# Moving transposes from TensorE to DMA and VectorE (32x32 blocks) in a fused two-layer graph kernel

## The chip, the cores and the metric

The kernel runs on one core of one Trainium2 chip. The metric is the device time of one execution in microseconds (us). The kernel before takes 2777.66 us (median of 3 runs, 2776.79 to 2779.71).

Names of engines in the profile: PE is TensorE's matmul, PEld its weight load, DVE is VectorE, ACT is ScalarE, POOL is GpSimd, SP is SyncE, which issues nearly all DMAs (all but 7 of 534 in the kernel before). A `q` behind an engine's name means its sequencer, which is where DMAs are issued. The granted clock is the share of TensorE's full speed that the profile shows; in the traces here it is either 1.00 or 0.50 (all 14 clock records of the kernel before), and figures between are means.

## The reference, cut to what matters

128 graphs of 128 nodes with 512 features go through an attention layer and a hypergraph layer. Only the first part matters for the change:

```python
# layer 0, per graph b and head h (8 heads of 64 units)
feats = einsum('bnf,hfu->bhnu', x, W)
dense = (feats . a_self)[..., :, None] + (feats . a_neigh)[..., None, :]
dense = leaky_relu(dense, 0.2) + NEG_BIG * (1 - adj)
att   = softmax(dense)                       # over neighbours j
out   = einsum('bhij,bhju->bhiu', att, feats) + b
x     = layernorm(x + relu(out))
# layer 1: y = R @ relu(R @ x @ W1 + b1) ..., R = D^-1 H B^-1 H^T with H = (adj != 0)
```

In this program each product on TensorE sums over the index that lies on the partitions of its operands. So `feats` takes x transposed (`xT`) and the weighted sum over j takes the exponentials transposed (`eT`); the degrees B, which VectorE sums along rows, take adj transposed (`hT`).

## The kernel before

Graphs are handled in 64 pairs. The large products are done with seven half-size products in place of eight; ScalarE copies some of the partial results out of PSUM and VectorE adds them. Each step is registered with a lag (how many pairs behind it works) and a position in the period. The positions are sorted once, and that order is the program order of every engine. The program is unrolled.

```python
    @step(0, 37.9)
    def transposes(p, s):                  # TensorE: x
        ...
                nc.tensor.transpose(t[:, k * P:(k + 1) * P], s["x"][:, g, k * P:(k + 1) * P], ident)
    def x_evict(p, s, g):                  # ScalarE: PSUM -> xT
        nc.scalar.copy(s["xT"][:, g].rearrange("p k n -> p (k n)"), s["pt"][g])
    ...
    @step(2, 21.6)
    def e_transpose(p, s):                 # TensorE: exponentials
        ...
                    nc.tensor.transpose(t[:, h * N:(h + 1) * N], s["nb"][:, g, q * HH + h, :], ident)
    def e_evict(p, s, g, q):               # ScalarE or VectorE: PSUM -> eT
        copy = (nc.scalar.copy, nc.vector.tensor_copy)[q]
        ...
    # what the argument needs besides
    at(3, 17.3, h_sum, 1, 0, 1, "W")       # VectorE: adds two partial results of ph
    at(3, 18.5, relu, 1, 0)                # ScalarE: ReLU of that sum
    # chain("pf", ...): ScalarE's copies of pfX stand behind it in ScalarE's order
    with tc.manual_schedule():
        for t in range(PAIRS + last):
            if 1 < t < PAIRS:
                load(t)
            ...
            for _, fn, args in sorted(todo, key=lambda e: e[0]):
                fn(*args)
```

In the profile `pz`, `ph`, `pf`, `pav`, `pr`, `py` and `pq` are TensorE's products in PSUM; `pf` gives the features, `pav` the weighted sums, `pr` the score rows. `nb` holds the scores, then the exponentials. A letter X, Y or W behind a product's name tells which PSUM bank collects it.

## Time and profile before

| what | kernel before | where it is read |
|---|---|---|
| time | 2777.66 us | median of 3 runs |
| TensorE busy | 98% of the span | busy shares of the page |
| chain of waits | 96% PE | the chain that ended last |
| one period (start of pz to the next) | 41.97 us | chain in order of time |
| busy in one period: PE, DVE, ACT, POOL | 42.0, 28.0, 26.3, 26.7 us | table of stretches |
| share of the DMA engines | 18% | queue table |

The first two rows say that TensorE bounds the kernel. The period turns a saving into a time: a microsecond taken out of every period is worth 64 us, as long as TensorE stays the bound. The lines themselves are in the prediction below.

### The profile page before, as it was taken

What the parts mean: (1) busy time and instruction counts of PE and PEld (TensorE: products, weight loads), DVE (VectorE), ACT (ScalarE), POOL (GpSimd) and SP (SyncE); (2) the same over time, 40 slices, a digit from 0 to 9 for tenths busy, and PEclk for the clock granted to TensorE, in tenths of its full rate; (3) what the DMA queues carried; (4) which work ended last, traced back from release to release, by engine and by line L of the source; (5) the groups of instructions that cost most, each with busy time, mean ns of one, the idle gap of its engine ahead of it and who ended that gap; (6) DMA issues with size and microseconds to landing.
All of it is one profiled execution on the core that took longest, in us unless ns stands there. A gap on an engine that the chain in (4) does not pass through costs nothing.

```text
span 2777.1 us, 50570 instructions
## 1 busy us (share of the span) xinstructions
PE 2713.2 (98%) x18272; PEld 2476.2 (89%) x18272; DVE 1796.3 (65%) x4264; ACT 1689.8 (61%) x4677; POOL 1725.9 (62%) x1813
## 2 busy tenths in 40 slices
PE   5799999999999999999999999999999999999997
PEld 4699999999999999999999999999999999999996
DVE  5566666666666666666666666666666666676663
ACT  2566566566566566666666665665665665665662
POOL 3665665666666666656656656656656656656654
PEclk8899999999999999999999999999999999999999
DMA  5111211211212212211212212212112112112110
GB/s 153 49 61 48 65 55 50 70 49 56 69 43 62 69 43 62 70 43 62 69 43 62 69 43 62 62 50 62 62 49 63 57 48 70 49 56 69 43 39 23
DMA packets 99660, 161.61 MB, mean 58 GB/s; under 512 B 11602, under 2 KB 48466, under 8 KB 99412
## 3 DMA queue, kind: packets, MB, share of 16 engines
q1 hardware_dynamic: 95716, 157.32, 18.0%
q8 instruction: 146, 2.39, 0.4%
q10 hardware_dynamic: 3696, 1.06, 0.2%
q14 instruction: 102, 0.84, 0.1%
HBM read 124.27 MB, written 34.08 MB: 57 GB/s over the span
## 4 chain that ended last, share of the span: by engine, by line
PE 96%; POOL 1%; DMA 1%; issue 1%; ACT 0%; DVE 0%; SPq 0%; POOLq 0%; DVEq 0%; ACTq 0%
PE phX L646 16%; PE pyX L404 16%; PE pfX L404 8%; PE phW L646 8%; PE pav L519 8%; PE pyW L404 8%; PE pz L610 4%; PE pfW L404 4%; PE phY L646 4%; PE pyY L404 4%; PE pq L767 4%; PE pet L498 4%; PE pfY L404 2%; PE pt L312 2%; PE pd L364 1%; PE pa L323 1%
## 5 line engine op out<-in xcount | busy, mean ns | idle before, releaser
L459 POOL TENSOR_TENSOR nb<-nb,neg 128x512 f32<-128x512 f32 x256 | 347.7, 1380 | 92.9 <-DMA nb<-rd 90.9
L646 PEld LDWEIGHTS phX<-zS,w_sb 128*128 128x128 f32 x3072 | 364.5, 193 | 41.2 <-issue 31.3
L646 PE MATMUL phX<-zS,w_sb 128*128 128x128 f32 x3072 | 375.9, 276 | 10.4 <-ACT ph L271 10.4
L271 ACT COPY py<-pyX 128x257 f32<-128x257 f32 (+1 forms) x192 | 71.4, 372 | 501.3 <-PE pyX L404 500.2
L466 ACT ACTIVATE nb<-nb,ft 128x128 f32<-128x128 f32 x1024 | 326.8, 392 | 50.5 <-POOL nb L459 49.5
L697 POOL TENSOR_TENSOR sq<-sq 128x512 f32<-128x512 f32 (+2 forms) x384 | 311.4, 818 | 20.1
L676 ACT ACTIVATE h<-h,b_sb 128x128 f32<-128x128 f32 x768 | 244.6, 391 | 124.3 <-DVE h L661 124.3
L479 ACT ACTIVATE nb<-nb,nm 128x128 f32<-128x128 f32 x1024 | 313.0, 391 | 0.0
L566 POOL TENSOR_TENSOR rso<-veo,mhalf 128x2 f32<-128x2 f32 x64 | 44.9, 701 | 420.9 <-DVE veo L564 420.9
L386 POOL TENSOR_TENSOR hS<-h 128x512 f32<-128x512 f32 x128 | 160.1, 1272 | 180.9 <-ACT h L676 180.9
L404 PE MATMUL pyX<-w_sb,h 128*128 128x257 f32 (+1 forms) x1024 | 252.9, 389 | 0.4 <-ACT py L271 0.2
L404 PE MATMUL pyX<-w_sb,hS 128*128 128x257 f32 (+1 forms) x1024 | 244.5, 381 | 2.5 <-POOL hS L386 2.5
L550 DVE SCALAR_TENSOR_TENSOR y<-y,x 128x512 f32<-128x512 f32 x128 | 186.6, 1458 | 89.4 <-POOL y L543 89.4
L519 PE MATMUL pav<-ft,eT 128*128 128x65 f32 x2048 | 241.8, 273 | 2.0 <-ACT eT L506 1.9
L404 PE MATMUL pyW<-w_sb,hS 128*128 128x256 f32 x1024 | 242.7, 379 | 0.0
L519 PEld LDWEIGHTS pav<-ft,eT 128*128 128x128 f32 x2048 | 239.6, 193 | 2.4 <-ACT eT L506 2.1
L634 POOL TENSOR_TENSOR zS<-zT 128x256 f32<-128x256 f32 x128 | 95.1, 743 | 226.5 <-ACT zT L621 226.5
L404 PEld LDWEIGHTS pyX<-w_sb,hS 128*128 128x128 f32 x1024 | 194.7, 190 | 31.5 <-POOL hS L386 2.9
L404 PEld LDWEIGHTS pyW<-w_sb,hS 128*128 128x128 f32 x1024 | 193.3, 189 | 29.1 <-DVE y L729 1.1
L427 DVE TENSOR_TENSOR ft<-pf,pfW 128x264 f32<-128x264 f32 x128 | 55.0, 430 | 236.5 <-ACT pf L271 165.5
L404 PEld LDWEIGHTS pyX<-w_sb,h 128*128 128x128 f32 x1024 | 185.4, 191 | 21.9 <-ACT py L271 0.7
L472 DVE TENSOR_REDUCE nm<-nb 128x4 f32<-128x512 f32 x256 | 168.7, 678 | 31.0 <-ACT nb L466 30.1
(131 smaller groups left out, 6174.1 us busy)
## 6 DMA issues: line engine op xcount, KB each, us to landing
nb<-rd SPq DMA_DIRECT2D x128, 512.0 KB, 4.5
x<-in_x_dram SPq DMA_DIRECT2D x64, 512.0 KB, 5.7
out_dram<-o SPq DMA_DIRECT2D x64, 512.0 KB, 2.8
a<-in_adj_dram SPq DMA_DIRECT2D x64, 128.0 KB, 5.0
w<-in_adj_dram SPq DMA_DIRECT2D x128, 64.0 KB, 4.8
w_sb<-in_w1t_dram SPq DMA_DIRECT2D x3, 512.0 KB, 6.5
w_sb<-in_w2t_dram SPq DMA_DIRECT2D x3, 512.0 KB, 9.2
w_raw<-in_w_dram SPq DMA_DIRECT2D x4, 256.0 KB, 6.6
```

Of the source, the lines that this page charges most:

```text
L386: engine.tensor_tensor(t[:, i], in0, in1, op=op)
L404: nc.tensor.matmul(to[:, :n], lhs[:, k, :], rhs[:, k, :n], start=bool(start) and k == 0, stop=(k == nk - 1), skip_group_check=True,)
L459: nc.gpsimd.tensor_tensor(t, t, s["neg"][:, g, None, :].to_broadcast([P, HH, N]), op=ALU.add)
L466: nc.scalar.activation(t, t, AF.Prelu, bias=s["ft"][:, g, h, 0:1], alpha=SLOPE)
L472: nc.vector.tensor_reduce(s["nm"][:, g, hs], s["nb"][:, g, hs, :], AX.X, ALU.max, negate=True)
L479: nc.scalar.activation(t, t, AF.Exp, bias=s["nm"][:, g, h:h + 1])
L498: nc.tensor.transpose(t[:, h * N:(h + 1) * N], s["nb"][:, g, q * HH + h, :], ident)
L519: nc.tensor.matmul(t[:, h * (U + 1):(h + 1) * (U + 1)], s["eT"][:, g, q * HH + h, :], s["ft"][:, g, q * HH + h, 2:], start=True, stop=True,)
L550: nc.vector.scalar_tensor_tensor(y, y, 0.0, s["x"][:, g, :], op0=ALU.max, op1=ALU.add)
L646: nc.tensor.matmul(to[:, m * N:(m + 1) * N], w[:, k, m * P:(m + 1) * P], rhs[:, k, :], start=bool(start) and m == 0 and k == 0, stop=(k == ...
L676: nc.scalar.activation(dst[:, k, :], src[:, k, :], AF.Relu, bias=b1_sb[:, c:c + 1])
L697: nc.gpsimd.tensor_tensor(t[:, :n, :], t[:, :n, :], t[:, n:2 * n, :], op=ALU.add)
```

## The change

TensorE spends 2.84 us of each period on the transposes of x, adj and the exponentials. The change takes these away; the small ones of hD and of the score rows stay. x and adj are read twice from DRAM, once in rows and once with the 32x32 blocks already at their transposed places. The exponentials are written to DRAM and read back in the same manner. VectorE then transposes inside each block (0.69 us for 128x512 in the mean of the 256 transposes of the exponentials; every experiment that uses it gave a correct result). Many positions are moved to the new pace. The core of the diff:

```diff
+    def load_blocks(p):
+        s["xb"] = work.tile([P, 2 * NB, P], F32, tag="xb", name=f"xb_{p}")
+        rows = x[gs].rearrange("g (b n) (f c) -> f n (g b) c", b=NB, f=NB)
+        for f in range(NB):
+            nc.sync.dma_start(s["xb"][f * B:(f + 1) * B], rows[f])
+        ...  # the same for adj, into "ab": eight DMAs in all
-    @step(0, 37.9)
-    def transposes(p, s):
-        ...
+    def x_transpose(p, s, g):
+        nc.vector.transpose(s["xT"][:, g]..., s["xb"][:, g * NB:(g + 1) * NB]...)
+    at(1, 4.7, x_transpose, 0)
+    at(1, 5.3, x_transpose, 1)
     ...
+    def e_write(p, s, g):
+        s["ed", g] = dram.tile([P, NB, H * B], F32, tag="ed", name=f"ed_{p}_{g}")
+        nc.sync.dma_start(s["ed", g], s["nb"][:, g * NB:(g + 1) * NB]...)
+    def e_read(p, s, g):
+        s["eb", g] = work.tile([P, NB, H, B], F32, tag="eb", name=f"eb_{p}_{g}", bufs=2)
+        for b in range(NB):
+            nc.sync.dma_start(s["eb", g][b * B:(b + 1) * B]..., s["ed", g][:, b, :]...)
+    def e_transpose(p, s, g, q):
+        nc.vector.transpose(s["eT"][:, g, hs, :]..., s["eb", g][:, :, hs, :]...)
-        ((0, 0), 33.0, (1, 34.9), (1, 37.3), 9.5), ...
+        ((0, 0), 32.7, (1, 33.4), (1, 34.8), 3.0, 12.5), ((0, 1), 34.0, (1, 35.7), (1, 37.3), 4.7, 13.9),
+        ((1, 0), 35.2, (1, 37.9), (2, 2.0), 9.3, 19.8), ((1, 1), 36.4, (1, 39.0), (2, 2.7), 11.6, 20.6),
     ...
+            if 0 < t < PAIRS:
+                todo.append((6.0, load_blocks, (t,)))
```

(The six columns of the table are: which quarter, then the positions of masking, leaky ReLU, maximum, exponential and VectorE's transpose.)

More of the change, by code (lines that the diff above doesn't have):

```diff
@@ L73 @@
     PAIRS = G // 2
+    B = 32
+    NB = P // B
     const = ctx.enter_context(tc.tile_pool(name="const", bufs=1))
@@ L94, in load @@
             nc.sync.dma_start(s["w"][:, g, :], adj[2 * p + g, 0, :].partition_broadcast(P))
-        if p:
-            load_x(p)
-    def load_x(p):
+    def load_blocks(p):
         s = st[p]
-        s["x"] = work.tile([P, 2, F], F32, tag="x", name=f"x_{p}", bufs=3)
-        nc.sync.dma_start(s["x"], x[2 * p:2 * p + 2].rearrange("g n f -> n g f"))
+        gs = slice(2 * p, 2 * p + 2)
+        s["xb"] = work.tile([P, 2 * NB, P], F32, tag="xb", name=f"xb_{p}")
+        rows = x[gs].rearrange("g (b n) (f c) -> f n (g b) c", b=NB, f=NB)
+        for f in range(NB):
+            nc.sync.dma_start(s["xb"][f * B:(f + 1) * B], rows[f])
+        s["ab"] = work.tile([P, 2 * NB, B], F32, tag="ab", name=f"ab_{p}")
+        rows = adj[gs].rearrange("g (b n) (f e) -> f n (g b) e", b=NB, f=NB)
+        for f in range(NB):
+            nc.sync.dma_start(s["ab"][f * B:(f + 1) * B], rows[f])
     load(0)
@@ L119 @@
         raw = work.tile([P, KF // 2, QU], F32, tag=("eT", "nb", "sq", "hS")[2 * i + j], name=f"w0_raw{i}{j}")
-        block(raw, w0, i, j, F // 2, QU)
+        rows = w0.rearrange("(b k f) c -> b f k c", b=NB, k=KF)
+        for b in range(NB):
+            nc.sync.dma_start(
+                raw[b * B:(b + 1) * B],
+                rows[b][:, i * KF // 2:(i + 1) * KF // 2, j * QU:(j + 1) * QU],
+            )
         w0_blocks.append((dst, raw.rearrange("p k (h u) -> p k h u", h=HH), j))
@@ L129 @@
     an_bc = spread(a_neigh, F, "an_bc")
-    load_x(0)
+    load_blocks(0)
     load(1)
@@ L180, in prepare_first @@
                 t = work.tile([P, KF // 2, HH, U], F32, tag=("o", "x")[c], name=f"wa{n}{c}",
-                              bufs=(2, 3)[c])
+                              bufs=2)
                 (nc.vector, nc.gpsimd)[c].tensor_tensor(
@@ L276, in chain @@
             at(lag, t, copy, i)
-    @step(0, 10.4)
+    @step(0, 9.2)
     def nodes(p, s):
@@ L284, in nodes @@
         dd = small.tile([P, 2], F32, tag="dd", name=f"dd_{p}")
-        junk = work.tile([P, N], F32, tag="junk", name=f"junk_{p}")
+        w = s["w"]
         for g in range(2):
             nc.vector.scalar_tensor_tensor(
-                junk, a[:, g, :], 0.0, s["w"][:, g, :], op0=ALU.not_equal, op1=ALU.mult,
+                w[:, g, :], a[:, g, :], 0.0, w[:, g, :], op0=ALU.not_equal, op1=ALU.mult,
                 accum_out=dd[:, g:g + 1],
@@ L299, in nodes @@
             )
-    @step(0, 38.3)
+    @step(0, 38.4)
     def mask(p, s):
@@ L304, in mask, with load_rows @@
         nc.gpsimd.tensor_scalar(s["neg"], s["a"], -1.0, BIG, op0=ALU.add, op1=ALU.mult)
-    @step(0, 37.9)
-    def transposes(p, s):
-        s["pt"] = []
-        for g in range(2):
-            t = bank(f"pt_{p}_{g}")
-            for k in range(KF):
-                nc.tensor.transpose(
-                    t[:, k * P:(k + 1) * P], s["x"][:, g, k * P:(k + 1) * P], ident
-                )
-            s["pt"].append(t)
-    @step(1, 1.75)
+    @step(1, 1.78)
     def transpose_nodes(p, s):
         s["pa"] = bank(f"pa_{p}")
-        for i, t in enumerate((s["a"], s["hD"])):
-            for g in range(2):
-                c = (2 * i + g) * N
-                nc.tensor.transpose(s["pa"][:, c:c + N], t[:, g, :], ident)
-    def x_evict(p, s, g):
+        for g in range(2):
+            nc.tensor.transpose(s["pa"][:, g * N:(g + 1) * N], s["hD"][:, g, :], ident)
+    @step(1, 31.0)
+    def load_rows(p, s):
+        s["x"] = work.tile([P, 2, F], F32, tag="x", name=f"x_{p}", bufs=2)
+        nc.sync.dma_start(s["x"], x[2 * p:2 * p + 2].rearrange("g n f -> n g f"))
+    def x_transpose(p, s, g):
         if g == 0:
             s["xT"] = work.tile([P, 2, KF, N], F32, tag="xT", name=f"xT_{p}")
-        nc.scalar.copy(s["xT"][:, g].rearrange("p k n -> p (k n)"), s["pt"][g])
-    at(0, 38.5, x_evict, 0)
-    at(0, 39.1, x_evict, 1)
+        nc.vector.transpose(
+            s["xT"][:, g].rearrange("p k (b n) -> p k b n", b=NB),
+            s["xb"][:, g * NB:(g + 1) * NB].rearrange("p b (k f) -> p k b f", k=KF),
+        )
+    at(1, 4.7, x_transpose, 0)
+    at(1, 5.3, x_transpose, 1)
     @step(1, 2.6)
@@ L335, in d_evict @@
         s["hDT"] = work.tile([P, 2, N], F32, tag="hDT", name=f"hDT_{p}")
-        nc.scalar.copy(s["hDT"].rearrange("p g n -> p (g n)"), s["pa"][:, 2 * N:])
-    @step(1, 2.4)
+        nc.scalar.copy(s["hDT"].rearrange("p g n -> p (g n)"), s["pa"][:, :2 * N])
+    @step(1, 3.4)
     def edges(p, s):
@@ L342, in edges @@
         hT = work.tile([P, 2, N], F32, tag="hT", name=f"hT_{p}")
+        nc.vector.transpose(hT.rearrange("p g (b n) -> p (g b) n", b=NB), s["ab"])
         for g in range(2):
             nc.vector.tensor_scalar(
-                hT[:, g, :], s["pa"][:, g * N:(g + 1) * N], 0.0, None, op0=ALU.not_equal,
-                op1=ALU.add, accum_out=deg[:, g:g + 1],
+                hT[:, g, :], hT[:, g, :], 0.0, None, op0=ALU.not_equal, op1=ALU.add,
+                accum_out=deg[:, g:g + 1],
             )
@@ L350, in edges @@
         s["hT"], s["be"] = hT, deg
-    @step(1, 16.5)
+    @step(1, 18.6)
     def scale_edges(p, s):
@@ L358, in scale_edges @@
             )
-    @step(1, 25.15)
+    @step(1, 34.6)
     def propagator(p, s):
@@ L367, in propagator @@
             )
-    @step(1, 25.9)
+    @step(1, 35.3)
     def r_evict(p, s):
@@ L394 @@
     for i in range(4):
-        at(1, 6.0 + 0.7 * i, x_sums, i)
+        at(1, 6.1 + 0.7 * i, x_sums, i)
     def rows_product(s, i, a, sums, w, n, nk, extra, to, start):
@@ L413, in feature @@
                      w0_sb.rearrange("p b k h u -> p b k (h u)"), FW, KF // 2, 0, to, start)
-    chain("pf", 1, (17.1, 18.0, 18.9, 19.8, 20.7, 23.35, 24.25, 18.15, 19.95, 21.75),
+    chain("pf", 1, (16.2, 17.1, 18.0, 18.9, 19.8, 22.4, 23.3, 17.3, 19.0, 20.8),
           feature, FW)
@@ L427, in f_sum @@
             nc.vector.tensor_tensor(dst, by_head(s["pf", i]), by_head(s["pf", where]), op=ALU.add)
-    at(1, 19.2, f_sum, 0, 0, 0, "Y")
-    at(1, 22.3, f_sum, 1, 1, 2, "W")
-    at(1, 25.3, f_sum, 0, 1, 1, "W")
-    at(1, 24.5, f_sum, 1, 0, None, "X")
-    @step(1, 27.3)
+    at(1, 18.2, f_sum, 0, 0, 0, "Y")
+    at(1, 21.4, f_sum, 1, 1, 2, "W")
+    at(1, 24.4, f_sum, 0, 1, 1, "W")
+    at(1, 23.4, f_sum, 1, 0, None, "X")
+    @step(1, 25.95)
     def transpose_scores(p, s):
@@ L439, in transpose_scores @@
         )
-    @step(1, 27.6)
+    @step(1, 26.2)
     def spread_rows(p, s):
@@ L445, in spread_rows, with neighbours, scores @@
         nc.vector.tensor_copy(rows, s["pr"][:2 * H, :N])
-        rd = dram.tile([2, H, N], F32, tag="rd", name=f"rd_{p}")
-        nc.sync.dma_start(rd.rearrange("g h n -> (g h) n"), rows)
-        s["nb"] = work.tile([P, 2, H, N], F32, tag="nb", name=f"nb_{p}")
+        rd = s["rd"] = dram.tile([2, NB, H, B], F32, tag="rd", name=f"rd_{p}")
         for g in range(2):
             nc.sync.dma_start(
-                s["nb"][:, g].rearrange("p h n -> p (h n)"),
-                rd[g].rearrange("h n -> (h n)").partition_broadcast(P),
-            )
+                rd[g].rearrange("b h j -> h b j"),
+                rows[g * H:(g + 1) * H].rearrange("h (b j) -> h b j", b=NB),
+            )
+    @step(1, 28.0)
+    def neighbours(p, s):
+        s["nb"] = work.tile([P, 2 * NB, H, B], F32, tag="nb", name=f"nb_{p}")
+        for g in range(2):
+            nc.sync.dma_start(
+                s["nb"][:, g * NB:(g + 1) * NB].rearrange("p b h j -> p (b h j)"),
+                s["rd"][g].rearrange("b h j -> (b h j)").partition_broadcast(P),
+            )
+    def scores(s, g, hs):
+        return s["nb"][:, g * NB:(g + 1) * NB, hs, :]
     def masked(p, s, g, q):
-        t = s["nb"][:, g, q * HH:(q + 1) * HH, :]
+        t = scores(s, g, slice(q * HH, (q + 1) * HH))
+        neg = s["neg"][:, g].rearrange("p (b j) -> p b j", b=NB)
         nc.gpsimd.tensor_tensor(
-            t, t, s["neg"][:, g, None, :].to_broadcast([P, HH, N]), op=ALU.add
+            t, t, neg[:, :, None, :].to_broadcast([P, NB, HH, B]), op=ALU.add
         )
@@ L464, in leaky @@
         for h in range(q * HH, (q + 1) * HH):
-            t = s["nb"][:, g, h, :]
+            t = scores(s, g, h)
             nc.scalar.activation(t, t, AF.Prelu, bias=s["ft"][:, g, h, 0:1], alpha=SLOPE)
@@ L472, in largest @@
         nc.vector.tensor_reduce(
-            s["nm"][:, g, hs], s["nb"][:, g, hs, :], AX.X, ALU.max, negate=True
+            s["nm"][:, g, hs], scores(s, g, hs).rearrange("p b h j -> p h b j"), AX.XY,
+            ALU.max, negate=True,
         )
@@ L477, in exponential @@
         for h in range(q * HH, (q + 1) * HH):
-            t = s["nb"][:, g, h, :]
+            t = scores(s, g, h)
             nc.scalar.activation(t, t, AF.Exp, bias=s["nm"][:, g, h:h + 1])
-    for (g, q), tm, (lag, tl), (lagx, tx), te in (
-        ((0, 0), 33.0, (1, 34.9), (1, 37.3), 9.5), ((0, 1), 34.3, (1, 36.2), (1, 38.3), 10.8),
-        ((1, 0), 35.6, (1, 40.6), (2, 3.5), 12.6), ((1, 1), 36.9, (2, 2.9), (2, 4.3), 13.9),
+    def e_write(p, s, g):
+        s["ed", g] = dram.tile([P, NB, H * B], F32, tag="ed", name=f"ed_{p}_{g}")
+        nc.sync.dma_start(
+            s["ed", g], s["nb"][:, g * NB:(g + 1) * NB].rearrange("p b h j -> p b (h j)")
+        )
+    def e_read(p, s, g):
+        s["eb", g] = work.tile([P, NB, H, B], F32, tag="eb", name=f"eb_{p}_{g}", bufs=2)
+        for b in range(NB):
+            nc.sync.dma_start(
+                s["eb", g][b * B:(b + 1) * B].rearrange("p i h j -> p i (h j)"),
+                s["ed", g][:, b, :].rearrange("(b i) x -> i b x", b=NB),
+            )
+    def e_transpose(p, s, g, q):
+        if (g, q) == (0, 0):
+            s["eT"] = work.tile([P, 2, H, N], F32, tag="eT", name=f"eT_{p}")
+        hs = slice(q * HH, (q + 1) * HH)
+        nc.vector.transpose(
+            s["eT"][:, g, hs, :].rearrange("p h (b i) -> p h b i", b=NB),
+            s["eb", g][:, :, hs, :].rearrange("p b h j -> p h b j"),
+        )
+    for (g, q), tm, (lag, tl), (lagx, tx), te, tt in (
+        ((0, 0), 32.7, (1, 33.4), (1, 34.8), 3.0, 12.5), ((0, 1), 34.0, (1, 35.7), (1, 37.3), 4.7, 13.9),
+        ((1, 0), 35.2, (1, 37.9), (2, 2.0), 9.3, 19.8), ((1, 1), 36.4, (1, 39.0), (2, 2.7), 11.6, 20.6),
     ):
@@ L488 @@
         at(2, te, exponential, g, q)
-    @step(2, 21.6)
-    def e_transpose(p, s):
-        for g in range(2):
-            for q in range(2):
-                t = s["pet", g, q] = bank(f"pet_{p}_{g}{q}")
-                for h in range(HH):
-                    nc.tensor.transpose(
-                        t[:, h * N:(h + 1) * N], s["nb"][:, g, q * HH + h, :], ident
-                    )
-    def e_evict(p, s, g, q):
-        if (g, q) == (0, 0):
-            s["eT"] = work.tile([P, 2, H, N], F32, tag="eT", name=f"eT_{p}")
-        copy = (nc.scalar.copy, nc.vector.tensor_copy)[q]
-        copy(
-            s["eT"][:, g, q * HH:(q + 1) * HH, :].rearrange("p h n -> p (h n)"), s["pet", g, q]
-        )
-    at(2, 22.6, e_evict, 0, 0)
-    at(2, 22.75, e_evict, 0, 1)
-    at(2, 23.5, e_evict, 1, 0)
-    at(2, 23.6, e_evict, 1, 1)
+        at(2, tt, e_transpose, g, q)
+        if q:
+            at(2, te + 1.6, e_write, g)
+            at(2, te + 3.6, e_read, g)
     def attend(p, s, g):
@@ L522, in attend @@
                 )
-    at(2, 25.6, attend, 0)
-    at(2, 27.4, attend, 1)
+    at(2, 20.65, attend, 0)
+    at(2, 24.2, attend, 1)
     def attended(p, s, g):
@@ L537, in attended @@
             )
-    at(2, 27.8, attended, 0)
-    at(2, 29.4, attended, 1)
+    at(2, 22.5, attended, 0)
+    at(2, 26.4, attended, 1)
     def add_bias(p, s, g):
         nc.gpsimd.tensor_tensor(s["y"][:, g, :], s["y"][:, g, :], b0_bc, op=ALU.add)
-    at(2, 29.9, add_bias, 0)
-    at(2, 31.2, add_bias, 1)
+    at(2, 24.1, add_bias, 0)
+    at(2, 28.0, add_bias, 1)
     def residual(p, s, g):
@@ L572, in normalize @@
         )
-    at(2, 31.3, residual, 0)
-    at(2, 33.2, residual, 1)
-    at(2, 35.5, rstds, "a")
-    @step(2, 36.3)
+    at(2, 27.6, residual, 0)
+    at(2, 30.0, residual, 1)
+    at(2, 31.7, rstds, "a")
+    @step(2, 32.6)
     def first_shift(p, s):
@@ L589, in first_output @@
         )
-    at(2, 39.7, first_output, 0)
-    at(2, 39.8, first_output, 1)
+    at(2, 37.0, first_output, 0)
+    at(2, 37.1, first_output, 1)
     def skip(p, s, g):
@@ L600, in skip @@
         )
-    at(3, 9.0, skip, 0)
-    at(3, 9.7, skip, 1)
+    at(3, 6.6, skip, 0)
+    at(3, 6.7, skip, 1)
     def propagate(p, s, g):
@@ L620, in z_evict @@
             s["zT"] = work.tile([P, 2, KF, N], F32, tag="zT", name=f"zT_{p}")
+            s["zS"] = work.tile([P, 4, KF // 2, N], F32, tag="zS", name=f"zS_{p}")
         nc.scalar.copy(s["zT"][:, g].rearrange("p k n -> p (k n)"), s["pz", g])
     at(3, 1.1, z_evict, 0)
-    at(3, 1.95, z_evict, 1)
+    at(3, 2.0, z_evict, 1)
     def z_sums(p, s, i):
-        if i == 0:
-            s["zS"] = work.tile([P, 4, KF // 2, N], F32, tag="zS", name=f"zS_{p}")
         b, t = halves(s["zT"], KF // 2), s["zS"]
@@ L634, in z_sums @@
         nc.gpsimd.tensor_tensor(t[:, i], in0, in1, op=ALU.subtract)
-    for i, t in enumerate((2.6, 3.3, 4.0, 4.7)):
+    for i, t in enumerate((2.7, 3.4, 4.1, 4.8)):
         at(3, t, z_sums, i)
@@ L650, in hidden @@
                 )
-    chain("ph", 3, (3.06, 4.81, 6.56, 8.31, 10.06, 13.56, 15.31, 4.9, 8.9, 12.0), hidden,
+    chain("ph", 3, (2.0, 3.8, 5.6, 7.35, 9.1, 12.65, 14.4, 4.0, 7.5, 11.0), hidden,
           HALF)
@@ L663, in h_sum @@
         )
-    at(3, 6.75, h_sum, 0, 0, 0, "Y")
-    at(3, 12.8, h_sum, 1, 1, 2, "W")
-    at(3, 17.3, h_sum, 1, 0, 1, "W")
+    at(3, 5.9, h_sum, 0, 0, 0, "Y")
+    at(3, 11.8, h_sum, 1, 1, 2, "W")
+    at(3, 16.4, h_sum, 1, 0, 1, "W")
     def relu(p, s, g, q):
@@ L676, in relu @@
             nc.scalar.activation(dst[:, k, :], src[:, k, :], AF.Relu, bias=b1_sb[:, c:c + 1])
-    at(3, 15.2, relu, 1, 1)
-    at(3, 16.5, relu, 0, 1)
-    at(3, 18.5, relu, 1, 0)
-    at(3, 7.6, relu, 0, 0)
+    at(3, 12.8, relu, 1, 1)
+    at(3, 14.5, relu, 0, 1)
+    at(3, 17.7, relu, 1, 0)
+    at(3, 8.1, relu, 0, 0)
     def square(p, s, g, q):
@@ L688, in square @@
         )
-    for (g, q), t in (((0, 0), 20.3), ((0, 1), 20.9), ((1, 0), 24.8), ((1, 1), 26.3)):
+    for (g, q), t in (((0, 0), 19.4), ((0, 1), 20.0), ((1, 0), 21.2), ((1, 1), 21.8)):
         at(3, t, square, g, q)
@@ L700 @@
         for level in range(3):
-            at(3, (25.0, 26.3, 27.0)[level] + 2.4 * g, squares, g, level)
+            at(3, (25.4, 26.7, 27.4)[level] + 3.9 * g, squares, g, level)
     def h_sums(p, s, i):
@@ L705, in h_sums @@
                    nc.gpsimd, "hS")
-    at(3, 21.1, h_sums, 0)
-    at(3, 22.4, h_sums, 1)
-    at(3, 19.8, h_sums, 2)
-    at(3, 23.7, h_sums, 3)
+    at(3, 20.3, h_sums, 0)
+    at(3, 21.6, h_sums, 1)
+    at(3, 19.0, h_sums, 2)
+    at(3, 22.8, h_sums, 3)
     def weigh(s, i, to, start):
         rows_product(s, i, halves(s["h"], KH // 2), s["hS"], w2_sb, QU, KH // 2, 1, to, start)
-    chain("py", 3, (29.2, 30.95, 32.7, 34.4, 36.2, 39.2, 40.9, 31.0, 34.5, 38.0), weigh,
+    chain("py", 3, (26.0, 27.8, 29.5, 31.2, 33.0, 35.5, 37.2, 27.9, 31.4, 34.75), weigh,
           QU, 1)
@@ L729, in y_sum @@
             nc.vector.tensor_tensor(dst, s["py", i][:, :n], s["py", where][:, :n], op=ALU.add)
-    at(3, 32.75, y_sum, 0, 0, 0, "Y")
-    at(3, 38.4, y_sum, 1, 1, 2, "W")
+    at(3, 29.6, y_sum, 0, 0, 0, "Y")
+    at(3, 35.4, y_sum, 1, 1, 2, "W")
     at(4, 0.1, y_sum, 0, 1, 1, "W")
-    at(3, 40.2, y_sum, 1, 0, None, "X")
-    @step(3, 38.8)
+    at(3, 37.3, y_sum, 1, 0, None, "X")
+    @step(3, 35.0)
     def sum_squares(p, s):
@@ L742, in sum_squares @@
             )
-    @step(3, 39.3)
+    @step(3, 36.0)
     def h_rstd(p, s):
@@ L769, in output @@
         )
-    at(4, 11.81, output, 0)
-    at(4, 12.7, output, 1)
+    at(4, 10.9, output, 0)
+    at(4, 11.8, output, 1)
     def o_sum(p, s, g):
@@ L779, in o_stats @@
         moments(p, s, "o", s["o"][:, g, :], g)
-    at(4, 13.4, o_sum, 0)
-    at(4, 14.1, o_sum, 1)
-    at(4, 14.8, o_stats, 0)
-    at(4, 15.6, o_stats, 1)
-    at(4, 15.7, rstds, "o")
-    @step(4, 18.2)
+    at(4, 12.7, o_sum, 0)
+    at(4, 13.3, o_sum, 1)
+    at(4, 14.7, o_stats, 0)
+    at(4, 15.5, o_stats, 1)
+    at(4, 15.6, rstds, "o")
+    @step(4, 17.1)
     def o_norm(p, s):
@@ L790, in o_norm @@
             normalize(s, "o", s["o"][:, g, :], g)
-        nc.sync.dma_start(
-            out[2 * p:2 * p + 2].rearrange("g n f -> n g f"), s["o"]
-        )
+        nc.sync.dma_start(out[2 * p:2 * p + 2].rearrange("g n f -> n g f"), s["o"])
     steps.sort(key=lambda e: e[:2])
@@ L799 @@
         0: [(11.0, prepare_first, ())],
-        1: [(2.5, prepare_first_sums, ()), (27.7, prepare_hidden, ())],
+        1: [(3.7, prepare_first_sums, ()), (26.3, prepare_hidden, ())],
         2: [(9.0, prepare_output, ()), (9.1, prepare_output_sums, ()),
             (41.5, prepare_output_blocks, (slice(0, 4),))],
-        3: [(8.8, prepare_output_block_sums, ())],
+        3: [(8.9, prepare_output_block_sums, ())],
     }
     def shift(t, lag, time):
-        if t == 1 and lag == 0 and time > 30.0:
-            return 25.2 - 37.9
-        if t == 2 and lag == 1 and time < 30.0:
-            return -17.0
-        return 0.0
+        return -17.0 if t == 2 and lag == 1 and time < 27.0 else 0.0
     with tc.manual_schedule():
         for t in range(PAIRS + last):
+            todo = list(once.get(t, ()))
             if 1 < t < PAIRS:
                 load(t)
-            todo = list(once.get(t, ()))
+            if 0 < t < PAIRS:
+                todo.append((6.0, load_blocks, (t,)))
             for time, _, lag, fn in steps:
```

## The prediction

> **What bounds the kernel now.** I read the page's busy shares first, then the row of the TensorE clock, then the chain of waits for one period, then the other engines in that period.

> ```profile
> span 2777.1 us, 50570 instructions
> PE 2713.2 (98%) x18272; PEld 2476.2 (89%) x18272; DVE 1796.3 (65%) x4264; ACT 1689.8 (61%) x4677; POOL 1725.9 (62%) x1813
> PEclk8899999999999999999999999999999999999999
> ```

> TensorE works 98% of the span at full clock; VectorE, ScalarE and GpSimd are idle for a third of it. The chain that ended last is 96% PE. In order of time it repeats every 41.95 us (one pair of graphs, 64 pairs); the pieces that the change touches are

> ```profile
> 1008.56 0.87 PE pt L312 x8
> 1013.34 1.78 PE pz L610 x16
> 1015.13 0.44 PE pa L323 x4
> 1015.56 1.79 PE phX L646 x16
> 1034.24 1.75 PE pet L498 x16
> 1055.31 1.78 PE pz L610 x16
> ```

> The pieces follow each other without a gap: 1055.31 - 1013.34 = 41.97 us, and 64 x 41.95 = 2685, so 92 us are filling and draining. A TensorE instruction taken out is worth its time, if nothing else gets in the way. One period of the others, from the table of stretches (1013.3 to 1055.3), sums to

> ```profile
> sum 42.00, PE 42.00 PEld 38.48 DVE 27.98 ACT 26.33 POOL 26.73; mean PE 3.82 PEld 3.50 DVE 2.54 ACT 2.39 POOL 2.43
> ```

> [...] No run so far shows such a transpose. [...] The trace before has comparable passes: the copy of 128x512 below takes 692 ns, and I take 0.69 us for a 128x512 transpose (an estimate) and 0.43 for 128x256. [...] SyncE waits for the small write before it issues the read of it (74.3 us in 64 waits, 1.16 each). [...] after 1.85 us idle the clock was 0.50 for 6.5 us.

> ```profile
> 2711.55 6.01 PE L519 MATMUL pav<-ft,eT 128*128 128x65 f32 x32 [1.85 <-ACT eT L506]
> 2713.00:2719.50 6.50, 6.50 (x27) 6.13 (x27) 2.16 (x7) 0.03 (x1) 6.19 (x7) 0.50 0.00 0
> ```

> **The change, part by part.** *TensorE*: gone are the 16 transposes of exponentials (1.75 us), 8 of x (0.87) and 2 of the 4 in pa (0.22): 2.84 us a period, 182 us in all, and nothing is added. Its own bound becomes 39.1 us.

> *ScalarE* loses four 128x512 evictions of about 0.587: 26.3 to 24.0 us. *VectorE* loses two evictions,

> ```profile
> L506 DVE COPY eT<-pet 128x512 f32<-128x512 f32 x128 | 88.4, 692 | 13.1 <-PE pet L498 11.2
> ```

> and gains six 128x512 transposes and one of 128x256: 27.98 - 1.38 + 6 x 0.69 + 0.43 = 31.2 us of 39.1, 80%. It fits as a sum; GpSimd is unchanged.

> *DMA*: x and adj are read twice (once by rows, once in blocks of 512 and 128 bytes), and the exponentials go out and back, 1 MB each way. One pair moved some 2.4 MB; now it is some 5 MB, and the 18% share of the DMA engines goes to about 50 to 60% (small blocks are slower: around 1044 us the 512-byte rows of adj moved at 180 to 190 GB/s with full engines, where x in 2 KB rows moved at 356 to 401). A sum that fits as well.

> What doesn't fit is, I think, the order. SyncE issues all DMAs in program order, and each issue costs it about 0.4 us:

> ```profile
> 1031.46 0.39 SPq L791 DMA_DIRECT2D out_dram<-o  x1
> 1041.98 0.81 SPq L450 DMA_DIRECT2D nb<-rd  x2
> 1043.36 0.89 SPq L94 DMA_DIRECT2D w<-in_adj_dram  x2
> ```

> A period had 8 issues and now has 27. The order of the built program shows on SyncE: 8 block loads of x and adj, then the write of the first graph's exponentials, its four reads, the write and the reads of the second. The block loads have a single buffer, so the first waits for VectorE's x transposes of the pair before. I walk through a period, 0 being the start of pz, with durations of the trace:

> 1. VectorE: y_sum and two scalings to 1.8 (as in the trace before), two maxima to 3.2, the adj transpose and the degrees (0.43 + 1.2) to 4.9, two x transposes to 6.3.
> 2. SyncE: eight block issues from 6.4, 8 x 0.4 = 3.2, so the exponentials' write is issued at 9.6. They have been ready since about 7.
> 3. The write is as large as that of the output, 2.8 us to landing: 12.4 if the engines are free. The block loads are 0.65 MB in small pieces, by the rate above some 5 us of all engines from 7.3; behind those it lands at about 15.
> 4. The four reads, 0.5 MB in 1 KB pieces: x as 2 KB rows had its data from 1.2 to 3.0 us after the issue; with four issues I take 3.6 to 4.1. Landing at 16.0 to 19.1.
> 5. VectorE stands at the first e_transpose from 12.6. From there its program order runs: transpose, two o_sums, transpose, statistics of o, h_sum(1,0): 0.69 + 1.36 + 0.69 + 2.0 + 0.69 = 5.5 us, so h_sum ends at 21.5 to 24.6.
> 6. ScalarE stands at the ReLU of that sum (four of 0.32), and only behind it copies pfX: 23.2 to 26.3.
> 7. TensorE needs that copy for the fifth product of pf. Without waits it gets there at 16.2 + 4 x 0.9 = 19.8. It stands for 3.4 to 6.5 us, say 5.0.

> Such a wait also lowers the clock. In the fill and drain, idle gaps of 1.85 to 10 us were followed by 3 to 7 us of work at 0.50; about 4.5 us at half speed lose 2.2. Since part of what runs slowly would wait for VectorE anyway, I count 1.3. Period: 39.1 + 5.0 + 1.3 = 45.4 us. The start has 16 loads for w0 in place of 4 and later x, say 10 us more. Sum: 64 x 45.4 + 92 + 10 = 3008 us.

> **The rivals.** *The plan works*: the new positions in the program match the new TensorE pace within 0.1 us (2.0, 3.8, 5.6 for the ph products, which the trace spaces at 1.79), so somebody has tuned with care, and a careful tuner would have seen a stall of 5 us. If DMA issues or landings of blocks are shorter than I think, or the walk's VectorE times too long, TensorE remains the bound at 39.1: 2777 - 182 + 10 = 2605. Against it: steps 2 to 4 rest on measured issues and landings, and even without any contention they give 3.4 us. *A small wait eats the gain*: if the round trip is 2 to 3 us late and the gap is too short to lower the clock, the period is 41 to 42.5 and the time 2725 to 2825. *VectorE or GpSimd becomes the bound*: at 80% and 68% not by sum; but both-SBUF operations such as y<-y,x already take 1458 ns where others take 690, and the masking now runs over inner rows of 32. It would add up to 1 us a period to any account, 64 us. *DMA bandwidth is the bound*: not at 50 to 60%.

> **Range and chances.** I give the stalled account 0.63 (centre 3008, width about 100), the small wait 0.13, the working plan 0.24 (about 2605). Weighted: 0.63 x 3008 + 0.13 x 2775 + 0.24 x 2605 = 2881. I put the point at 2900, nearer to the main account; the range must take in the edge of the working plan and the long stall: 2630 to 3100. Faster by over 2% means below 2722: 0.25. Slower means above 2833: 0.63. Within: 0.12.

> **What would show it.** In the changed kernel's chain of waits: PE's share below 90%, with pieces of DMA eb<-ed, DVE eT and ACT h and pf. In the waits: VectorE at eT for the DMA that writes eb, 3 to 6 us each period; ScalarE's ReLU for DVE h; TensorE's pfX for ACT pf. The clock row would show 8s or 7s. SyncE's issues of xb and ab should be eight in a row of about 0.4 us, just before ed<-nb. The transpose group should read about 690 ns. I am wrong if eb lands before VectorE reaches eT (then the period is near 39.1), if the chain stays above 95% PE, or if a transpose of 128x512 takes over 1 us, which would make VectorE the bound by its sum.

## The result, and the profile after

The changed kernel takes 3139.86 us (median of 4 runs, 3134.54 to 3146.95) beside 2777.82 us of the kernel before: the ratio is 1.1304, with a 95% interval of 1.1275 to 1.1334. A ratio here is always the mean time of one kernel's fast runs over the mean of the other's from the same rounds, so it is not quite the ratio of the medians. The direction was predicted. The time is 240 us above the point and 40 us above the range. All outputs are right.

The page of the changed kernel, with the engines' busy time and the granted TensorE clock in 40 slices:

```profile
span 3145.2 us, 48588 instructions
PE 2797.0 (89%) x16608; PEld 2488.0 (79%) x16608; DVE 2015.1 (64%) x4584; ACT 1520.4 (48%) x4421; POOL 1748.1 (56%) x1813
PEclk8889889889999889898998998898999988999998
...
PE 30%; DVE 20%; DMA 19%; POOL 12%; ACT 8%; issue 6%; SPq 5%; DVEq 0%; POOLq 0%
```

TensorE runs 1664 instructions fewer and yet is busy 84 us longer (2797.0 against 2713.2). That is only possible if the same instructions have become slower, and the clock row shows why: 18 of its 40 slices are at 8 (rounded down to tenths), where before only the first two were; the mean clock is 0.911 in place of 0.991. PE's share of the chain fell from 96% to 30%.

The chain of waits in order of time (start, duration, what) shows one pass through the new path. The period begins with pz at 1533.84:

```profile
1538.49 1.21 DVE xT L338 x2
...
1543.61 4.02 DMA ed<-nb
...
1548.94 2.81 DMA eb<-ed
...
1551.88 0.71 DVE eT L527
...
1556.17 0.60 DVE h L692
1556.80 1.28 ACT h L707 x4
1558.08 0.27 ACT pf L289
...
1558.48 1.40 PE pfX L418 x4
```

TensorE's fifth pf product (1558.48) starts as the last link of a chain that begins with VectorE's transposes of x. The chain runs through the write of the exponentials, the read, VectorE's first transpose, the sum h behind it, the ReLU, and a copy. (Up to the write, the view names GpSimd's sums xS, left out above, because they end at that moment. The write doesn't need them: SyncE's order, below, is what it waits for, and in e1_loads_late it goes out before they end.) The waits over the whole run (engine and line, what it waited for; us in total, times, longest) say that this is so in every period:

```profile
DVE eT L527 <- DMA eb<-ed: 300.6, 65, 8.6
ACT h L707 <- DVE h L692: 274.7, 65, 5.9
PE pfX L418 <- ACT pf L289: 235.2, 63, 5.3
```

That is 4.6, 4.2 and 3.7 us a period: one delay, handed from engine to engine. What it does to TensorE is seen in its timeline (start, us, ...; in brackets the idle time before and what ended it), in two lines of the stretch table (window; us; busy PE, PEld, DVE, ACT, POOL; clock; DMA share; GB/s), and in the sum of the period 1533.84 to 1581.60:

```profile
1558.48 1.40 PE L418 MATMUL pfX<-w_sb,xS 128*128 128x264 f32 x4 [4.22 <-ACT pf L289]
1559.67 3.52 PE L551 MATMUL pav<-ft,eT 128*128 128x65 f32 x16
```

```profile
1560.00:1561.00 1.00, 1.00 (x6) 1.00 (x7) 1.00 (x2) 1.00 (x3) 0.92 (x2) 0.50 0.32 123
1565.00:1566.00 1.00, 1.00 (x4) 0.79 (x3) 0.00 (x0) 0.38 (x1) 1.00 (x2) 0.50 0.00 0
```

```profile
sum 47.76, PE 43.10 PEld 38.53 DVE 31.21 ACT 23.69 POOL 27.09; mean PE 5.39 PEld 4.82 DVE 3.90 ACT 2.96 POOL 3.39
```

The first pav takes 3.52 us; the one that follows at full clock takes 1.90. The clock is 0.50 from about 1559.2 to 1566.0, which is 6.8 us. VectorE's and ScalarE's sums, 31.2 and 23.7 us, are what was predicted (31.2 and 24.0), so neither is the bound. The mean period is 47.72 us, and 64 of them make 3054 of the 3145 us span.

SyncE's issues in the same period (start, duration of the issues, line, what, count):

```profile
1539.71 1.81 SPq L109 DMA_DIRECT2D xb<-in_x_dram  x4
1541.57 1.93 SPq L114 DMA_DIRECT2D ab<-in_adj_dram  x4
1543.61 1.74 SPq L510 DMA_DIRECT2D ed<-nb  x1
1547.64 1.73 SPq L518 DMA_DIRECT2D eb<-ed  x4
```

The exponentials were ready at 1540.06, the end of ScalarE's exponential. Their write was issued 3.55 us later, behind eight block loads of 0.47 us each that had just been freed by the transposes of x: over the whole run SyncE stands 893.1 us, in 62 waits, at the first block load until those transposes are done. In most periods the write's own issue is shorter than here (0.38 us in the median of 50 periods, not 1.74), so the reads go out at 12.6 us; VectorE's first transpose starts at 17.7.

### The profile page after: what moved, and what is told of

Same layout as the page of the kernel before. It is cut to its first block, busy times and chain, and to the rows that moved or that the text cites. A ratio compares the mean times of both kernels' runs of the same rounds, so it can differ in the third digit from the quotient of the medians.

```text
span 3145.2 us, 48588 instructions
## 1 busy us (share of the span) xinstructions
PE 2797.0 (89%) x16608; PEld 2488.0 (79%) x16608; DVE 2015.1 (64%) x4584; ACT 1520.4 (48%) x4421; POOL 1748.1 (56%) x1813
## 3 DMA queue, kind: packets, MB, share of 16 engines
q8 instruction: 132, 2.16, 0.3%
## 4 chain that ended last, share of the span: by engine, by line
PE 30%; DVE 20%; DMA 19%; POOL 12%; ACT 8%; issue 6%; SPq 5%; DVEq 0%; POOLq 0%
PE pav L551 10%; PE pfX L418 7%; DMA eb<-ed 6%; DMA a<-in_adj_dram 6%; DMA ed<-nb 6%; POOL xS L400 4%; PE pyX L418 4%; POOL y L575 3%; PE pyW L418 3%; ACT nb L492 3%; PE pfW L418 3%; ACT h L707 3%; DVE eT L527 3%; SPq L518 3%; POOL sq L728 2%
## 5 line engine op out<-in xcount | busy, mean ns | idle before, releaser
L551 PEld LDWEIGHTS pav<-ft,eT 128*128 128x128 f32 x2048 | 360.8, 264 | 32.8 <-issue 13.6
L418 PE MATMUL pfX<-w_sb,xS 128*128 128x264 f32 x512 | 173.0, 469 | 234.3 <-ACT pf L289 234.3
L527 DVE STREAM_TRANSPOSE eT<-eb 128x512 f32<-128x512 f32 x256 | 172.4, 692 | 300.6 <-DMA eb<-ed 300.6
L551 PE MATMUL pav<-ft,eT 128*128 128x65 f32 x2048 | 346.6, 342 | 12.9 <-DVE eT L527 12.9
L728 POOL TENSOR_TENSOR sq<-sq 128x512 f32<-128x512 f32 (+2 forms) x384 | 335.1, 873 | 20.1
L485 POOL TENSOR_TENSOR nb<-nb,neg 128x512 f32<-128x512 f32 x256 | 320.2, 1273 | 15.1 <-DMA nb<-rd 15.1
L506 ACT ACTIVATE nb<-nb,nm 128x128 f32<-128x128 f32 x1024 | 327.2, 396 | 0.0
L418 PEld LDWEIGHTS pfX<-w_sb,xS 128*128 128x128 f32 x512 | 107.2, 221 | 275.3 <-issue 257.8
L575 POOL TENSOR_TENSOR y<-y,b_bc 128x512 f32<-128x512 f32 x128 | 185.3, 1448 | 214.0 <-DVE y L566 213.9
L498 DVE TENSOR_REDUCE nm<-nb 128x4 f32<-128x512 f32 x256 | 169.2, 682 | 100.0 <-ACT nb L492 94.2
L418 PE MATMUL pfX<-w_sb,xT 128*128 128x264 f32 x512 | 196.5, 522 | 30.3 <-DVE xT L338 29.3
```

Of the source, the lines that this page charges most:

```text
L418: nc.tensor.matmul(to[:, :n], lhs[:, k, :], rhs[:, k, :n], start=bool(start) and k == 0, stop=(k == nk - 1), skip_group_check=True,)
L485: nc.gpsimd.tensor_tensor(t, t, neg[:, :, None, :].to_broadcast([P, NB, HH, B]), op=ALU.add)
L498: nc.vector.tensor_reduce(s["nm"][:, g, hs], scores(s, g, hs).rearrange("p b h j -> p h b j"), AX.XY, ALU.max, negate=True,)
L506: nc.scalar.activation(t, t, AF.Exp, bias=s["nm"][:, g, h:h + 1])
L527: nc.vector.transpose(s["eT"][:, g, hs, :].rearrange("p h (b i) -> p h b i", b=NB), s["eb", g][:, :, hs, :].rearrange("p b h j -> p h b j"),)
L551: nc.tensor.matmul(t[:, h * (U + 1):(h + 1) * (U + 1)], s["eT"][:, g, q * HH + h, :], s["ft"][:, g, q * HH + h, 2:], start=True, stop=True,)
```

## The experiments

Theory: the eight issues ahead of the write make the round trip late; VectorE stands in order at the first transpose; the sum, the ReLU and the copy behind it are late; TensorE waits about 4 us; and the wait halves the clock for longer than I had counted. Rivals were that the round trip itself, its traffic, or some other sum is the bound.

### The loads behind the round trip (e1_loads_late)

```diff
-                todo.append((6.0, load_blocks, (t,)))
+                todo.append((15.3, load_blocks, (t,)))
```

> Only the place of the eight block loads changes: from before the write of the first graph's exponentials to behind the second graph's reads. Theory (order): SyncE then issues the write as soon as the exponentials are there, some 6.3 us after the start of pz instead of 9.8; it lands 2.7 us later, the reads 4.2 us after that, at about 13.4, where VectorE arrives at 12.9. TensorE waits under 1 us, its clock stays at 1.00, the period is 39.5 to 41 us in place of 47.8 and the time 2600 to 2720 us, so faster than both kernels. Rival (traffic: twice the bytes and three times the packets cost wherever they stand, or the VectorE transposes do): the time stays above 2950 us.

Measured: 2737.75 us (2734.87 to 2739.46), ratio to the kernel before 0.9856 (0.984 to 0.9872), clock 0.987. SyncE's issues now read, in a period that begins at 1501.54:

```profile
1507.81 0.33 SPq L510 DMA_DIRECT2D ed<-nb  x1
1510.92 1.75 SPq L518 DMA_DIRECT2D eb<-ed  x4
...
1519.45 1.85 SPq L109 DMA_DIRECT2D xb<-in_x_dram  x4
```

The write goes out 6.3 us into the period where it had been 9.8, and TensorE's wait for the pf copy falls from 235.2 us in all to 15.2:

```profile
PE pfX L418 <- ACT pf L289: 15.2, 26, 1.1
```

One line of the program is worth 402 us against the changed kernel, so the loss came from where the loads stood, not from the round trip as such. The time is 18 us above the expected range, though the median period of 40.96 us lies in it (39.5 to 41): the mean is 41.23, and the first pz starts at 94.5 us, 17.6 later than in the kernel before. The waits show TensorE at the third py copy 62 times for 0.64 us; ScalarE has the leaky ReLUs in front of that copy. That is what the last experiment below takes up.

### Useless products in the gap (e2_fill_gap)

```diff
+    @step(1, 19.75)
+    def keep_clock(p, s):
+        t = bank(f"warm_{p}")
+        for k in range(16):
+            nc.tensor.matmul(t[:, :P], w1_sb[:, 0, 0, :P], ident, start=True, stop=True)
```

> The changed kernel with 16 useless matmuls of 128x128 (32 TensorE records, 3.6 us at full clock) put where TensorE waits, before the fifth product of pf; they write a bank that nobody reads. Theory (clock): the 4.2 us of idling are followed by 6.8 us at half clock, which costs 3.4 us a period; with the gap filled the clock stays at 1.00, and the kernel with more work is faster: 3140 - 60 x 3.4 = 2935 us, between 2900 and 2980. Rival (the low clock has another cause, or the added work comes on top): 3140 us or more.

Measured: 2975.61 us (2973.17 to 2978.59), ratio 1.0717 (1.0701 to 1.0733), clock 0.989. TensorE's timeline in one period:

```profile
1516.96 3.73 PE L433 MATMUL warm<-ident,w_sb 128*128 128x128 f32 x32
...
1521.42 1.89 PE L557 MATMUL pav<-ft,eT 128*128 128x65 f32 x16
```

Nothing waits less for the exponentials (VectorE stands at eT for 296.1 us in all, nearly the 300.6 of the changed kernel), TensorE has 3.6 us more to do in each period, and the kernel is 164 us faster than the changed one, inside the expected range. The pav behind the gap takes 1.89 us in place of 3.52. So the idle time itself costs clock here, and the clock is a large part of the loss: the period is 44.87 us in place of 47.87 (medians).

### Only the part of x and adj (e3_x_adj_only)

The kernel before with the diff's `load_blocks`, `x_transpose` and the transpose of `ab` alone; the exponentials stay on TensorE.

> The kernel before with only the x and adj part of the change: block loads and VectorE transposes for x and adj, the exponentials still by TensorE and evictions. Theory: this part has nothing that waits for a round trip, TensorE stays the bound at 41.95 - 0.87 - 0.22 = 40.86 us a period, time 64 x 40.86 + 100 = 2715 us (2690 to 2740), clock 1.00. Rival (the blocks' small packets or the x transposes on VectorE do the harm): above 2777 us.

Measured: 2753.46 us (2751.43 to 2756.38), ratio 0.9917 (0.9902 to 0.9932), clock 0.99. PE still has 96% of the span and 80% of the chain. This part does no harm, but it brings 23 us and not the 63 that I had expected, 13 us above the range: about 10 us are lost at the start, and the median period in the profile is 41.29 us where 40.88 would be the old one (41.97) less 1.09 us of transposes. TensorE waits for the third py copy in 62 periods, 0.25 us each.

### Only the part of the exponentials (e4_exp_only)

The changed kernel without `load_blocks`; x and adj are transposed by TensorE as before.

> The changed kernel with only the exponentials through DRAM and VectorE; x and adj by TensorE as before, no block loads. Theory (the block loads before the write are what makes the round trip late): without them the write is issued at about 6.5 us, the data are there at about 13.5, TensorE is the bound at 39.1 + 1.09 = 40.2 us a period, time 2640 to 2720 us. Rival (the round trip through DRAM is itself too long for this place): a wait at the fifth product of pf, lower clock, time above 2800 us.

Measured: 2777.95 us (2776.87 to 2780.31), ratio 1.0005 (0.999 to 1.002), clock 0.99: a miss of 58 us above the range. The round trip without block loads ahead of it does not stop TensorE (20.1 us at pfX in the whole run, none of the half clock), so the theory's main point held. But the saved 1.75 us of each period came to nothing, as the waits of TensorE show:

```profile
PE phX L669 <- ACT zT L646: 53.7, 62, 0.9
```

In each period 0.87 us go to the eviction of zT, which stands behind leaky ReLUs in ScalarE's order, and ScalarE has the two evictions of x besides. In the medians of 50 periods, beside the kernel before, TensorE loses 1.14 us around that wait and 0.42 us at the sixth and seventh pf product, together 1.56 of the 1.75; what holds up the latter was not looked into. So neither half of the change loses anything by itself; they lose together.

### VectorE's transposes later in its order (e7_transposes_later)

```diff
-  ((0, 0), ..., 12.5), ((0, 1), ..., 13.9), ((1, 0), ..., 19.8), ((1, 1), ..., 20.6),
+  ((0, 0), ..., 16.5), ((0, 1), ..., 17.2), ((1, 0), ..., 21.45), ((1, 1), ..., 21.5),
```

> The changed kernel with only VectorE's program order changed: the four transposes of the exponentials stand behind h_sum(1,0) and f_sum(1,1) instead of at 12.5, 13.9, 19.8 and 20.6. Loads, ring traffic and the time at which the exponentials land are as in the changed kernel. Theory (VectorE standing in order at the first transpose holds up h_sum, ReLU and the pf copy, and so TensorE): the wait of pfX for the copy goes, the clock stays at full speed, the period falls from 47.8 to 41 to 42.5 us, time 2720 to 2850. Rival (the late round trip itself is the bound, because attend needs eT whoever waits for it): TensorE now waits at pav instead of at pfX, the half clock stays, time 3000 or more. Mean clock: theory 0.98 or more, rival 0.93 or less.

Measured: 2777.07 us (2770.92 to 2777.46), ratio 0.9994 (0.9978 to 1.0011), clock 0.978, mean period 41.84 us: time and period as the theory expected, the clock just under its 0.98. The loads still stand ahead of the write. The waits of TensorE are now

```profile
PE pyX L418 <- ACT py L289: 92.0, 62, 1.9
...
PE pav L551 <- DVE eT L527: 16.1, 9, 7.9
...
PE pfX L418 <- ACT pf L289: 0.9, 2, 0.5
```

The wait at pfX is gone, and hardly any at pav has come in its place (16.1 us in the whole run, most of it in the start). In a period that begins at 1521.73 the first two transposes end at 19.7 us, and pav is reached at 21.1. What stopped TensorE was the work that stood behind the transpose in VectorE's order, not the want of `eT`. The round trip itself did not change: the write goes out at 9.76 us and the reads at 12.60 in the median of 50 periods, in both kernels. What is left is again the third py copy, 1.5 us a period; after it the clock still halved for 3.4 us in 15 periods.

### The loads between the write and the reads (e8_loads_between)

```diff
-                todo.append((6.0, load_blocks, (t,)))
+                todo.append((7.0, load_blocks, (t,)))
```

> The changed kernel with the eight block loads issued behind the first write of exponentials and ahead of its four reads, instead of ahead of both; the loads still meet the round trip on the DMA engines. In the changed kernel's trace the exponentials are ready 6.2 us after the start of pz and the write is issued at 9.8, behind eight issues of 0.47 us. Theory (the order of issue on SyncE is what delays the round trip): the write is issued at about 6.4, the reads at about 10.5, and eb lands at 14 to 15 instead of 18.0; TensorE's wait falls from 4.2 us to about 1 and the clock stays at full speed; period 40.8 to 42.5, time 2740 to 2830. Rival (the loads' packets on the shared DMA engines are what delays it): the write or the reads land late all the same, eb at 17 or later, TensorE waits over 3 us and the clock falls again; time 3000 or more.

Measured: 3016.97 us (3010.72 to 3026.06), ratio 1.0873 (1.0847 to 1.0898), clock 0.932. This is a miss: the number falls in the rival's range. SyncE in a period that begins at 1505.56:

```profile
1511.84 0.33 SPq L510 DMA_DIRECT2D ed<-nb  x1
1512.21 3.18 SPq L109 DMA_DIRECT2D xb<-in_x_dram  x4
1515.43 1.93 SPq L114 DMA_DIRECT2D ab<-in_adj_dram  x4
1517.40 1.87 SPq L518 DMA_DIRECT2D eb<-ed  x4
```

The write goes out at 6.3 as I had said. But the reads now stand behind the eight issues, and those take 5.15 us, not 3.8, because one of them was held up by 1.3 us while the write's data moved (4.4 in the median of 50 periods). The reads go out at 11.8 without any wait for the write, and eb is there at 16.1 (the end of the read in the chain of waits). So the queue order on SyncE decided again, on the reads this time, with a smaller share of the traffic on top: both theories had a part, and I had overlooked that moving the loads behind the write puts them before the reads. The legs of the round trip (medians of 50 periods) tell the shares apart. In the changed kernel VectorE's first transpose starts 4.0 us later than in e1_loads_late (17.70 against 13.74); 3.5 of that is the later issue of the write, while the leg from the write to the reads (2.84 against 2.65) and the one from the reads to the transpose (5.10 against 4.81; 5.14 here) bring 0.5, the most that traffic can account for. TensorE's wait is 2.3 us a period (147.5 us in 63), and even that halved the clock: after 2.44 us of idle time the stretches read

```profile
1529.00:1530.00 1.00, 1.00 (x4) 0.79 (x3) 1.00 (x2) 0.33 (x1) 1.00 (x2) 0.50 1.00 387
...
1532.00:1533.00 1.00, 1.00 (x9) 1.00 (x9) 0.75 (x4) 0.00 (x0) 0.98 (x1) 1.00 0.00 0
```

The cost is not in proportion to the wait. From the fifth pf product to pr, 6.2 us at full clock, four successive periods took 7.9, 9.6, 6.6 and 7.9 us, after idle times of 2.44, 2.43, 1.89 and 2.36 us. Over the 61 steady periods of the run, idle times of 1.6 to 3.6 us were followed by no half clock at all in 22, and by 3.4, 6.8 or 10.2 us of it in the others, where the same work took up to 11.2 us.

### Loads late, and four positions more (e5_retuned)

```diff
-    @step(1, 18.6)
+    @step(1, 12.3)
     def scale_edges(p, s):
-  ((0, 0), 32.7, (1, 33.4), ...), ... ((1, 1), 36.4, (1, 39.0), (2, 2.7), 11.6, 20.6),
+  ((0, 0), 32.7, (1, 34.8), ...), ... ((1, 1), 36.4, (2, 4.9), (2, 6.5), 11.6, 20.6),
-                todo.append((6.0, load_blocks, (t,)))
+                todo.append((15.3, load_blocks, (t,)))
```

> The version with the block loads behind the round trip (e1_loads_late), and in addition three positions in program order: the leaky steps of (0,0) behind the third copy of py, those of (1,1) behind both evictions of zT, and the scaling of hB before GpSimd's hS sums. Theory: what e1_loads_late lost above the TensorE sum of 39.1 us were small waits on ScalarE's and VectorE's order (0.65 us for the third py copy, 0.2 to 0.4 for zT, and about 1 us behind hB, which took 2.5 us beside GpSimd). Then the period is 39.3 to 40.0 us and the time 64 x 39.6 + 116 = 2650, range 2610 to 2700. Rival (some other resource bounds it, VectorE by its sum or GpSimd): the period stays at 40.7 to 41.0 and the time at 2720 to 2745.

Measured: 2676.19 us (2673.56 to 2677.57), ratio 0.9637 (0.9623 to 0.9651): faster than both kernels, and inside the expected range, as is the median period of 39.90 us. In one of the shortest periods (1506.83 to 1546.38) and in the waits of TensorE:

```profile
sum 39.55, PE 39.38 PEld 35.63 DVE 29.45 ACT 23.85 POOL 27.13; mean PE 39.38 PEld 35.63 DVE 29.45 ACT 23.85 POOL 27.13
```

```profile
PE pfX L418 <- ACT pf L289: 17.0, 29, 1.4
...
PE pyW L418 <- DVE y L760: 11.1, 62, 0.5
```

TensorE is the bound again, at 39.38 us of 39.55. The waits for the third py copy and for zT have left the list. VectorE's sum is 2.1 us less than in the period of e1_loads_late, which is mainly the scaling of hB: there its two instructions took 2.5 us beside GpSimd's sums (1.27 us each in the median of the run), here 0.47 (0.28 each in the median).

One more thing could not be tried: two buffers for the block loads, which would have let them go out before the transposes of x. The pool of work tiles would then need 119.6 KB a partition where 116.2 KB of SBUF were left, and the program did not build. Issuing the block loads from another engine's queue was not tried either.

## Why the prediction was right or wrong

**Steps 1 to 3, the issue and the write: right.** In the period shown the transposes of x ended at 5.84 us (predicted 6.3), the eight issues took 3.8 us (3.2), the write was issued at 9.8 (9.6) and landed at 13.8 (12.4 to 15). The rate behind the 15 was misread, though: by the DMA records of the kernel before, the packets around 1044 us are 4 KB pieces of nb<-rd, not rows of adj. Over that whole run a 512-byte packet took 27 ns in the median and a 2 KB one 84; a 128-byte packet of the changed kernel took 13.

**Steps 4 to 6, read, VectorE, ScalarE: right.** eb was there at 18.0 (16.0 to 19.1), the sum of h ended at 22.9 (21.5 to 24.6), the copy of pfX at 24.5 (23.2 to 26.3). The transposes of 128x512 took 0.69 us on average, as estimated from the copy of that size. e1_loads_late shows that the order of the loads is the cause, e7_transposes_later that the stand at eT, in VectorE's order, hands it on.

**Step 7, TensorE's wait: right.** 4.22 us in that period and 3.7 in the mean, where I said 3.4 to 6.5 and counted 5.0.

**The clock: the mechanism right, the term mis-sized, and this is the step that failed.** The prediction said "about 4.5 us at half speed lose 2.2. Since part of what runs slowly would wait for VectorE anyway, I count 1.3." The half clock lasted 6.8 us. The work from the fifth pf product (1558.48) to pr (1568.06) took 9.58 us; the same instructions take 6.19 us in the fully clocked e5_retuned, so 3.4 us were lost. The discount was wrong too: the timeline shows no further wait of TensorE between pfX and pr, so nothing of the slow work was hidden. Over 61 steady periods the half clock lasted 6.8 us in 32, 10.2 us in 27 and was absent in 2; the same work took 9.9 us on average, 3.7 more than in e5_retuned. The 4.5 us had come from the fill and drain of the kernel before. After gaps of 8.5 to 10.3 us there, part of the half clock lay inside the gap and only 3.2 to 4.4 us of it were left for work; after the gaps of 1.85, 2.53 and 3.52 us, nearer to the predicted 5.0, the work at half clock lasted 6.8, 3.4 and 6.0 us. e2_fill_gap shows the clock's part by itself.

**Left out: two short waits in ScalarE's order.** The eviction of zT and the third py copy cost TensorE 0.37 and 0.38 us in that period, compared with e5_retuned. I had walked only one stretch of the period. With 39.2 us for TensorE's own work (39.55 in e5_retuned, less 0.3 that it loses at pyW and the changed kernel doesn't), the period adds up: 39.2 + 4.2 + 3.4 + 0.8 = 47.6 of 47.76. My 45.4 was 0.8 too high on the wait, 2.1 too low on the clock and 0.8 too low on these.

**The range.** The main account, 3008, would have been 132 us off, about the 2.3 us of the period times 64. That account was then drawn down to 2900 by weight given to rivals. The upper edge of 3100 stood less than its width of 100 above the account that I believed in, although the clock, its most uncertain term, was in it at 1.3 us of the 2.2 that I had worked out.

**The rivals.** "The plan works" was refuted for the kernel as it was given, but it describes what the change could be: e5_retuned reaches 2676 against my 2605 for it. The difference is mainly a mean period of 40.2 in place of 39.1 (70 us), and a start that is 19 us longer where I allowed 10. "A small wait eats the gain" describes e4_exp_only and e7_transposes_later, both within 1 us of 2777.5. VectorE's sum, GpSimd's sum and the DMA share bound nothing; the last was 34% of the run where I had said 50 to 60. Why y<-y,x took 1458 ns was not shown: two other operations of that size with both operands in SBUF took 1067 (o<-y,b_bc) and 747 (y<-y,rsh,bw_bc) in the same run, and y<-y,x took 856 in the changed kernel.

## What to carry to other kernels

When work moves from a busy engine to DMA and an idle one, the sums can all fit and the kernel still lose: walk the new path in program order through the issuing queue and through every engine that stands and waits on it, and look at what stands behind each wait. Put prefetches behind the transfers that somebody is waiting for (402 us here, e1_loads_late), and an engine's wait behind the work that others need from it (363 us, e7_transposes_later). Count a wait of TensorE at more than its length: in the changed kernel an idle time of 3.8 us on average (2.9 to 5.3 in all but one period) cost another 3.7 us of half clock on average, and in e8_loads_between 1.6 to 3.6 us of idle time cost anything from nothing to 5.0 us.
